# Placing the side tasks of one projection at fixed steps, in a graph-attention layer on one core

## The chip, the core and the metric

The kernel runs on one core of a Trainium2 chip. Times are device microseconds (us) of whole executions. TensorE (PE) multiplies matrices, VectorE (DVE) and ScalarE (ACT) do elementwise work, GpSimd (POOL) does elementwise work and can also issue DMA transfers, SyncE (SP) issues most transfers. Everything is float32.

## The reference, cut to what matters

For each of 128 graphs of 64 nodes: layer norm and relu, four attention heads, a second attention over the joined heads, a feed-forward of two layers, a layer norm and the residual.

```python
Wh = einsum('bnf,hfo->bhno', x, W)
e = leaky_relu(f1[..., :, None] + f2[..., None, :])        # f1, f2: Wh times the two halves of a
attn = softmax(where(adj > 0, e, -1e9), axis=-1)
h = elu(attn @ Wh)                                         # four heads, then once more with W_out
y = relu(out @ w1 + b1) @ w2 + b2 + out
```

## The kernel before

The nodes are cut into 16 groups of four row tiles. Products are done with seven block products in place of eight, so there are weight sums and input sums, and many of them are GpSimd's work. One loop body handles the second projection of group `g` (28 steps on PE of 4 matmul calls each, which the trace lists as 8 instructions, and 1.73 us each) and slips in tasks of other groups. Group 0 has its own list, because the start of the kernel still has work to finish: the first attention of group 0, the softmax of group 1, loads and sums of the feed-forward weights `w1` (M1) and `w2` (M2), norms and softmax of group 2.

```python
def weight_sums(m, after=None):                 # GpSimd: four sums, then two stores of 512 KB
    free = [nc.gpsimd.tensor_tensor(s[0][:, 0], b12, b11, ALU.subtract)]        # L200
    nc.gpsimd.tensor_tensor(s[0][:, 1], b22, s[0][:, 0], ALU.subtract)          # L201
    free.append(nc.gpsimd.tensor_tensor(s[1][:, 0], b22, b12, ALU.subtract))    # L202
    ...
    last = nc.gpsimd.tensor_tensor(s[1][:, 1], b21, s[0][:, 1], ALU.subtract)   # L205
    ...
    for i in range(2):
        nc.gpsimd.dma_start(out=TC[m][i], in_=s[i])                             # L208

def fetch(m, after=None):                       # a whole weight, 1 MB
    queue = nc.scalar if m == 0 else nc.sync if m < H else nc.gpsimd
    ins = queue.dma_start(out=MT[m], in_=mats[m].rearrange("(k p) o -> p k o", p=P))   # L166
...
# softmax of the head weights, VectorE; ei is a tile in SBUF, pe one in PSUM
nc.vector.tensor_tensor(ei, pe[:, i:i + n], mask, ALU.add)                       # L429
nc.vector.scalar_tensor_tensor(ei, ei, ALPHA, ei, ALU.mult, ALU.max)             # L435
nc.vector.tensor_reduce(mi, ei, AX.X, ALU.max)                                   # L436
nc.vector.tensor_tensor(ei, ei, mi[...], ALU.subtract)                           # L437
...                                                                              # exp on ScalarE, sum, 1/sum
nc.vector.tensor_tensor(A[:, u, 0:H], ei[...], ri[...], ALU.mult)                # L443
nc.vector.tensor_copy(A[:, u, H], A[:, u, 0])                                    # L448
```

PE then transposes the weights `A` (L485), and the attention of group 1 is built from them. The other GpSimd work in the stage: L672 adds two blocks of the hidden values, L688 takes differences of blocks for the second projection (each waits until PE has read the block that it overwrites), L314 to L316 are sums of the attention's result `z`, L334 and L344 the scale and shift of a norm.

A scheduler orders each engine's instructions; the kernel steers it by the order of the calls and by `behind(ins, other, reason)`.

## Time and profile before

| | before |
|---|---|
| execution, median of 3 | 2320.97 us (2320.66 to 2322.14) |
| span of the profiled execution | 2318.7 us |
| PE busy | 2279.3 us, 98% |
| PE idle from 100 to 190 us | 16.9 us |
| granted PE clock from 100 to 190 us | 0.91 |

In a kernel in which PE is busy nearly always, a stretch of idle time can be seen only when one asks for PE's own waits. The idle time is the 90 us of that stretch less the 73.06 us in which PE is busy; 14.08 us of it are one gap. The prediction shows the lines.

### The profile page before, as it was taken

What the parts mean: (1) busy time and instruction counts of PE and PEld (TensorE: products, weight loads), DVE (VectorE), ACT (ScalarE), POOL (GpSimd) and SP (SyncE); (2) the same over time, 40 slices, a digit from 0 to 9 for tenths busy, and PEclk for the clock granted to TensorE, in tenths of its full rate; (3) what the DMA queues carried; (4) which work ended last, traced back from release to release, by engine and by line L of the source; (5) the groups of instructions that cost most, each with busy time, mean ns of one, the idle gap of its engine ahead of it and who ended that gap; (6) DMA issues with size and microseconds to landing.
All of it is one profiled execution on the core that took longest, in us unless ns stands there. A gap on an engine that the chain in (4) does not pass through costs nothing. (4 is left out here: it accounts for less than half of the span.)

```text
span 2318.7 us, 33251 instructions
## 1 busy us (share of the span) xinstructions
PE 2279.3 (98%) x11856; PEld 1893.2 (82%) x11856; DVE 1288.4 (56%) x2227; ACT 903.3 (39%) x1629; POOL 1017.0 (44%) x907
## 2 busy tenths in 40 slices
PE   8889999999999999999999999999999999999997
PEld 4568888888888888888888888888888888888885
DVE  7545475555646555475555646555465554744427
ACT  3425425253352534425254252533525244251512
POOL 7742544426344353444425444253443525533324
PEclk9989999999999999999999999999999999999999
DMA  7634454454545445454454545445453454635543
GB/s 277 222 110 134 134 183 136 155 162 134 182 132 177 132 146 178 135 181 132 146 175 133 185 133 159 155 139 181 134 177 130 148 177 132 182 119 165 166 146 105
DMA packets 255011, 361.14 MB, mean 156 GB/s; under 512 B 23768, under 2 KB 143608, under 8 KB 254848
## 3 DMA queue, kind: packets, MB, share of 16 engines
q1 hardware_dynamic: 249744, 341.16, 46.4%
q0 software_dynamic: 4576, 16.81, 2.0%
q8 instruction: 96, 1.57, 0.3%
q10 hardware_dynamic: 528, 1.05, 0.1%
q14 instruction: 67, 0.55, 0.1%
HBM read 331.66 MB, written 27.26 MB: 155 GB/s over the span
## 5 line engine op out<-in xcount | busy, mean ns | idle before, releaser
L304 PE MATMUL g_b<-w,h 128*128 128x256 f32 x2560 | 593.7, 379 | 0.0
L304 PEld LDWEIGHTS g_b<-w,h 128*128 128x128 f32 x2560 | 481.0, 190 | 65.0 <-issue 2.5
L289 PE MATMUL g_a<-z,w 128*128 128x256 f32 x1440 | 341.9, 380 | 0.0
L289 PE MATMUL g_a<-zs_z,w 128*128 128x256 f32 x1440 | 336.0, 381 | 0.0
L289 PEld LDWEIGHTS g_a<-zs_z,w 128*128 128x128 f32 x1440 | 269.9, 190 | 59.2 <-issue 24.3
L289 PEld LDWEIGHTS g_a<-z,w 128*128 128x128 f32 x1440 | 272.3, 190 | 41.3 <-DVE g_a L603 5.0
L304 PE MATMUL g_b<-w,hS 128*128 128x256 f32 x1024 | 240.0, 381 | 0.0
L607 POOL TENSOR_TENSOR hS<-hS,h 128x512 f32<-128x512 f32 x60 | 78.0, 1299 | 360.5 <-DVE hS L573 360.5
L304 PEld LDWEIGHTS g_b<-w,hS 128*128 128x128 f32 x1024 | 193.6, 192 | 25.3
L571 ACT ACTIVATE exc<-g_a 128x512 f32<-128x512 f32 x240 | 142.5, 594 | 163.7 <-DVE g_a L603 95.9
L573 DVE SCALAR_TENSOR_TENSOR h<-exc,g_a 128x512 f32<-128x512 f32 x180 | 123.5, 686 | 140.8 <-ACT exc L572 140.2
L572 ACT ACTIVATE exc<-exc 128x512 f32<-128x512 f32 x240 | 151.4, 631 | 6.6
L314 POOL TENSOR_TENSOR zs_z<-zS,z 128x512 f32<-128x512 f32 x60 | 85.1, 1419 | 139.4 <-PE g_a L289 135.5
L688 POOL TENSOR_TENSOR h<-h,h 128x512 f32<-128x512 f32 x64 | 86.8, 1364 | 135.1 <-PE g_b L304 135.1
L688 POOL TENSOR_TENSOR h<-hS,h 128x512 f32<-128x512 f32 x64 | 81.1, 1268 | 142.6 <-PE g_b L304 142.6
L489 ACT COPY at<-s1pt 128x512 f32<-128x512 f32 x64 | 34.6, 589 | 279.3 <-PE s1pt L485 279.3
L830 POOL TENSOR_TENSOR xr<-xr,bs 128x512 f32<-128x512 f32 x64 | 96.8, 1517 | 78.1 <-DMA xr<-in_x_dram 45.5
L304 PE MATMUL g_d<-w,rt 128*128 128x256 f32 x512 | 121.8, 380 | 2.3 <-DVE o L822 1.0
L289 PE MATMUL g_c<-ot,w 128*128 128x256 f32 x512 | 122.7, 382 | 0.6 <-DVE ot L792 0.6
L289 PE MATMUL g_a<-zS,w 128*128 128x256 f32 x480 | 113.4, 379 | 0.0
L304 PEld LDWEIGHTS g_d<-w,rt 128*128 128x128 f32 x512 | 96.9, 190 | 17.4 <-DVE o L822 2.3
L712 DVE SCALAR_TENSOR_TENSOR jf<-wh,ao 128x512 f32<-128x512 f32 x128 | 97.3, 795 | 24.3 <-ACT wh L694 24.2
(164 smaller groups left out, 3549.1 us busy)
## 6 DMA issues: line engine op xcount, KB each, us to landing
w<-tc SPq DMA_DIRECT2D x624, 256.0 KB, 2.6
w<-in_L_gnn_W_out_dram SPq DMA_DIRECT2D x192, 256.0 KB, 2.7
w<-in_L_gnn_W_heads_dram SPq DMA_DIRECT2D x180, 256.0 KB, 3.0
w<-in_L_gnn_w_dram SPq DMA_DIRECT2D x96, 256.0 KB, 2.7
x<-in_x_dram SPq DMA_DIRECT2D x64, 256.0 KB, 3.7
xr<-in_x_dram SPq DMA_DIRECT2D x128, 128.0 KB, 2.7
out_dram<-o SPq DMA_DIRECT2D x128, 128.0 KB, 2.4
tc<-pt POOLq DMA_DIRECT2D x20, 512.0 KB, 4.3
```

The lines of the kernel that those rows point to most:

```text
L289: LAST["pe"] = nc.tensor.matmul(bk[:, o, :], w[:, k, ts(o, P)], a[:, k, :], start=start and o == 0 and k == 0, stop=k == 1, skip_group_che ...
L304: LAST["pe"] = nc.tensor.matmul(bk[:, j, :], a[:, k, ts(j, P)], w[:, k, :], start=start and k == 0 and j == 0, stop=i == len(ms) - 1 and k ...
L314: eng.tensor_tensor(s2, s1, a11, ALU.subtract)
L489: nc.scalar.copy(AT[t].rearrange("p b h n -> p (b h) n"), pt)
L571: nc.scalar.activation(ex, src, AF.Relu, scale=-1.0)
L572: nc.scalar.activation(ex, ex, AF.Exp, scale=-1.0)
L573: nc.vector.scalar_tensor_tensor(dst, ex, -1.0, src, ALU.add, ALU.max)
L607: nc.gpsimd.tensor_tensor(dst, dst, H1["22"][:, h], ALU.add)
L688: nc.gpsimd.tensor_tensor(dst[:, h], x0[:, h], x1[:, h], ALU.subtract)
L712: nc.vector.scalar_tensor_tensor(junk, WH2[g][:, j], 1.0, ao[:, c, :], ALU.mult, ALU.mult, accum_out=f[:, c, j:j + 1],)
L830: nc.gpsimd.tensor_tensor(xr, xr, bs, ALU.add)
```

## The change

The intent: every side task gets the step of the product behind which it stands. The sums of `w1` go behind the softmax of group 1, the transposes of that softmax two steps later, the load and sums of `w2` later, the norms of group 2 ahead of the sums of `z`.

```diff
-        if g < 2:                                   # the factor R: ScalarE, else VectorE and GpSimd
+        if g < 3:
...
-                if t < G:                           # transposes not ahead of the last product step
+                if t < 2 * G:
...
-    sums_of(M1, LAST["hw", 3, 0])                   # load and sums
+    fetch(M1, LAST["hw", 3, 0])                     # the load alone
...
-        lambda: (attend0(2, 1), turn0(1, 1)), lambda: (attend0(3, 1), turn0(2, 1), project_f(1)),
-        lambda: turn0(3, 1), lambda: (scores1(1), attn_weights(2)), nothing, lambda: attn_weights(3),
-        lambda: (fetch(M2, LAST["hw", 3, 3]), weight_sums(M2, LAST["pe"])), nothing,
-    ] + turns[1:] + [nothing] * 2
...
+                2: lambda: (turn0(3, 1), scores1(1), attn_weights(2), attn_weights(3)),
+                5: lambda: weight_sums(M1, LAST["pe"]),
+                7: turns1[1],
+                8: lambda: fetch(M2, LAST["pe"]),
...
+                13: lambda: (attn[3](), norms[1]()),
+                15: scores[0],
+                16: scores[1],
+                17: lambda: weight_sums(M2, LAST["pe"]),
...
+                22: lambda: z_sums(g + 1, 0),
+                24: turns[1],
+                27: lambda: (turns[4](), load_rows()),
```

## The prediction

> **What bounds the kernel now.** First the page's busy table and its slices. TensorE (PE) is the bound almost everywhere, and the only weak spot ahead of the tail is in the first three slices (a slice is 2318.7 / 40 = 58 us); in the third, from 116 us, the granted clock is down too, to 8 tenths. So the question is where PE waits, not how busy the others are.
>
> ```profile
> PE 2279.3 (98%) x11856; PEld 1893.2 (82%) x11856; DVE 1288.4 (56%) x2227; ACT 903.3 (39%) x1629; POOL 1017.0 (44%) x907
> ...
> PE   8889999999999999999999999999999999999997
> ...
> PEclk9989999999999999999999999999999999999999
> ```
>
> Then the waits of PE alone, over the whole span. One wait dwarfs the rest: the transposes of the attention weights (L485) for the softmax's last multiply (L443). The 6.6 us is the kernel's start, which the change does not touch; the 2.4 us (transposes of normalized rows for a PSUM copy on ScalarE) lies in the same stage, the second projection of group 0.
>
> ```profile
> PE s1pt L485 <- DVE s1A L443: 14.3, 2, 14.1
> PE pab L177 <- DMA ar<-in_L_gnn_a_heads_dram: 6.6, 1, 6.6
> PE pth L362 <- ACT hT L364: 2.4, 1, 2.4
> PE g_c L289 <- ACT t_c L255: 1.1, 1, 1.1
> ```
>
> Then the order in time of PE, VectorE (DVE) and GpSimd (POOL) around that wait (columns: start, duration, engine, line, operation; the bracket is the idle time before it). PE:
>
> ```profile
> 106.37 3.62 PE L304 MATMUL g_b<-w,hS 128*128 128x256 f32 x16
> 124.06 1.94 PE L485 MATMUL s1pt<-ident,s1A 128*128 128x128 f32 x8 [14.08 <-DVE s1A L443]
> 125.80 4.64 PE L304 MATMUL g_b<-w,hS 128*128 128x256 f32 x16
> ...
> 162.08 1.97 PE L362 MATMUL pth<-ident,hn 128*128 128x128 f32 x8 [2.39 <-ACT hT L364]
> 163.84 2.67 PE L304 MATMUL g_b<-w,hS 128*128 128x256 f32 x8
> ```
>
> VectorE in the same time: the leaky-relu step of the softmax takes 14.76 us where the 32 of its line and shape have a median of 0.69.
>
> ```profile
> 105.36 14.76 DVE L435 SCALAR_TENSOR_TENSOR s1e<-s1e 128x512 f32<-128x512 f32 x1
> 120.16 0.69 DVE L436 TENSOR_REDUCE s1mx<-s1e 128x8 f32<-128x512 f32 x1
> ```
>
> GpSimd runs without any idle time from 103.66 to 119.5: differences of the hidden blocks (L672, L688) and the sums of a weight (L200 to L205). VectorE's step ends 0.6 us after the last of them.
>
> ```profile
> 103.66 1.28 POOL L688 TENSOR_TENSOR h<-hS,h 128x512 f32<-128x512 f32 x1
> ...
> 113.44 1.25 POOL L200 TENSOR_TENSOR pt<-pw 128x512 f32<-128x512 f32 x1
> ...
> 118.32 1.25 POOL L205 TENSOR_TENSOR pt<-pw,pt 128x512 f32<-128x512 f32 x1
> 119.53 1.10 POOL L208 DMA_DIRECT2D tc<-pt  x2
> ```
>
> **What the Trainium skill says.** "SBUF — State Buffer", section "Who interferes with whom": a VectorE instruction with two SBUF inputs contends with a GpSimd instruction that reads SBUF, and the one that comes second blocks fully. L435 reads the same SBUF tile twice, so it is of that kind; the 14.76 us beside 0.69 agrees. That it is passed over at twelve boundaries between GpSimd instructions is not what the page leads one to expect, nor usual here: in the later stages the two engines take turns (at 290.01 an L315 of VectorE took 1.64 us, one GpSimd instruction's length longer). "TensorE: Matmul & The Clock Gate", "What's actually happening": an idle window of about 3.4 us halves the clock, and about 3.4 us of work restores it. The trace agrees in kind: 8 transposes took 1.94 us after the wait and 1.04 elsewhere, 16 matmuls 4.64 and 3.62; the granted clock was 0.76 in 124.06 to 132. It also dropped (1.97 us for 8 transposes) after the 2.39 us wait.
>
> **What can be had.** From start to start, so that overlap is not counted twice, 16 matmuls take 3.45 us and 8 transposes 0.87.
> - First wait: 14.08 idle. Afterwards 124.06 to 125.80 is 1.74 for 0.87, and 125.80 to 130.28 is 4.48 for 3.45: 0.87 + 1.03 = 1.90 of slow clock.
> - Second wait: 2.39 idle; 1.76 for 0.87 and 2.60 for 1.73 afterwards: 1.76 (the rest, 0.1, is rounding of start-to-start).
> - Three small waits for the second pair of transposes (178 to 186 us): 0.18 + 0.14 + 0.14 = 0.46.
>
> - A slow issue that counts as busy: the 8 matmuls of the head product L641 at 95.02 take until 96.95, 1.93 where others take 1.02: 0.9.
>
> Sum 14.08 + 1.90 + 2.39 + 1.76 + 0.46 + 0.9 = 21.5 us. From 190 to 2261 us PE has no idle time of 0.1 us, the matmuls are the same number before and after, and from the next stage on the order of instructions is the same in both kernels. So the floor is 2321.0 - 21.5 = 2299.5 us, a gain of 0.9%. 2% would be 46 us, and is not there.
>
> **The change part by part.**
> 1. *The sums of the first feed-forward weight leave the front of the softmax.* Before, they hold GpSimd from 95.49 to 101.6 (four of 1.27 and two DMA issues of 0.55), so the four sums L672 and the differences L688, ready from about 87 us on, queue up behind them and then run as one block. In the changed order they stand behind the second difference of the fifth product. GpSimd then keeps up with PE, and each L688 waits for its own matmuls: PE steps take 1.73, the L688 takes 1.27, so there are holes of 0.4 us and more in which VectorE gets the port. My estimate with before's durations: scores are done at 103.7 instead of 104.5 (the same work stands in front of them, but the head product that was slow comes one step later), L435 starts at 104.5, waits for one L672 to 105.1, ends at 105.7; L437 ends at 107.5; L443 starts at about 109.1, takes turns with GpSimd and ends at 110.9, L448 at 112.2.
> 2. *Two more steps of the product go in front of the transposes.* Before, the transposes stand behind the second hS step; now behind the fourth. That is 2 x 1.73 = 3.45 us more cover: PE arrives at 109.2 + 3.45 = 112.6, after the softmax. First wait: 14.08 to about 0.
> 3. *The sums of the second weight go to step 17*, 4 x 1.25 + 1.1 = 6.1 us out of the block of 103 to 120. The first weight's sums take their place, though: three of them start at about 110.6, and run beside the second softmax of group 1. Its L435, L437, L443 and L448 then take turns, at 0.5 to 1.1 us each: it ends at about 120, against 122.5 at which PE wants it. But the copies of z stand behind it on VectorE, and PE wants one at 120.6. Left over: 0.3 us.
> 4. *Norms ahead of the sums of z.* Before, six z sums (7.5 us) and a L688 hold GpSimd until 158.6, the norms' scale comes after them, and ScalarE's copies wait for it; that is the 2.39. In the changed order both norms stand ahead of the six. From the end of step 13: statistics 1.7, GpSimd's four small ones 1.8, ScalarE to 4.4; PE wants the first transposes at 5.4, the next at 8.0. Second wait and its slow clock: 4.15 to 0.
> 5. *Group 2's factor R on ScalarE instead of VectorE and GpSimd*: four of 0.38 in place of 0.41 + 1.04, done 15.7 us after step 13, against 16.8 at which PE wants it. Nothing, but it keeps R from waiting behind the sums of the second weight.
> 6. Those sums fall at 15.1 to 20.1 us on that scale, and the softmax of group 2 begins at 17.8: 0.6 to 2 us of delay, of which the four steps in front of the transposes (6.9 us for a softmax of 5.5) hide 1.4. The second half has eight score products (L712, 0.68) woven in: 0.3 to 1.5 us of wait.
>
> Left over: 0 + 0.3 + about 1 = 1.3, and 0.3 for a transpose that follows its rows closely at 101.6: 2299.5 + 1.6 = 2301. Such countings leave out waits more often than they invent them, and so I add 3: **2304 us**.
>
> **Rivals.**
> - *VectorE is passed over again.* If L443 or the second L435 meets the first weight's sums and is passed over until they end at about 116.6, the transposes come at 118 instead of 112.6: 5.4 us and 1.9 of slow clock, 2308 to 2309. For: it happened at 105.36, and the sums start on a PE step, not on the softmax. Against: of the 128 instructions L712, also with two SBUF inputs, many beside GpSimd, the longest took 1.76.
> - *The wait moves to group 2*: part 6 goes to its worst, and a wait over 2.4 us costs clock too. 2304 to 2306.
> - *The wait is something else's*, weights not landed for instance, and the softmax was only last. Against: the fifth product's weights were issued at 90 to 93 us, and land in 2.6. 2317 or more; under 5%.
>
> **Range and chances.** Low end is the floor, rounded to 2299.5; the first rival with a little of the second gives the high end, 2310. Executions agree within 1.5 us (2320.66 to 2322.14), so noise adds little. Faster by over 2% would need twice what is idle; slower by over 2% would need a new wait of 46 us.
>
> **What would show it.** Right: no L435 of the first 200 us over 2.5 us; PE's wait for s1A from 14.3 to under 2; no wait for hT at the norms; the granted clock of 100 to 190 us from 0.91 to 0.98 or more; the next stage (g_a, now at 184.2) starting 16 to 20 us sooner, and the same distance at the end. Wrong: an L443 or L435 of 5 us or more that ends with a L205; idle PE in front of the second pair's transposes; a new wait for z.

## The result, and the profile after

The changed kernel took 2299.46 us (median of 4, 2298.54 to 2299.75), against 2320.81 for the kernel before with its newer run counted in. The ratio is 0.9907, 95% interval 0.9890 to 0.9924. A ratio is the mean time of one kernel's fast runs over that of the other's of the same rounds, so it is not quite the ratio of the medians. All outputs are right.

The page of the changed kernel: busy times, and the slices with the granted clock. Before, PE's row began with 888; of these three dips the first, which holds the kernel's start, is left. The dip of the clock is gone.

```profile
PE 2274.2 (99%) x11856; PEld 1892.9 (82%) x11856; DVE 1278.8 (56%) x2226; ACT 904.4 (39%) x1633; POOL 1019.9 (44%) x906
...
PE   8999999999999999999999999999999999999997
...
PEclk9999999999999999999999999999999999999999
```

PE's waits: what was 14.3 us for the softmax is 0.5, and the 2.4 us for ScalarE's copy is gone. The wait at the kernel's start is what it was.

```profile
PE pab L177 <- DMA ar<-in_L_gnn_a_heads_dram: 6.8, 1, 6.8
...
PE s1pt L485 <- DVE s1A L443: 0.5, 1, 0.5
```

PE in order of time. Four hS steps stand in one piece (32 matmuls) in front of the transposes, and nothing is idle: no bracket.

```profile
103.91 1.99 PE L304 MATMUL g_b<-w,h 128*128 128x256 f32 x8
105.74 7.07 PE L304 MATMUL g_b<-w,hS 128*128 128x256 f32 x32
112.65 1.04 PE L485 MATMUL s1pt<-ident,s1A 128*128 128x128 f32 x8
```

VectorE: L435 takes 1.09 us in place of 14.76. It and L437, L443 and L448 each wait for the end of one GpSimd instruction.

```profile
104.74 1.09 DVE L435 SCALAR_TENSOR_TENSOR s1e<-s1e 128x512 f32<-128x512 f32 x1
...
109.17 1.26 DVE L443 TENSOR_TENSOR s1A<-s1e,s1r 128x512 f32<-128x512 f32 x1
110.46 1.17 DVE L448 COPY s1A<-s1A 128x128 f32<-128x128 f32 x1
```

GpSimd: still no idle time that the view would put in a bracket, from 104.01 to 112.7 (pauses of 0.08 us get no bracket). But some of its instructions take 1.6 to 1.7 us, and not 1.27: those are the ones that waited for VectorE in their turn. The load of `w2`, which was issued at 102.86 before, is issued at 121.35.

```profile
104.01 1.27 POOL L688 TENSOR_TENSOR h<-hS,h 128x512 f32<-128x512 f32 x1
105.25 1.72 POOL L672 TENSOR_TENSOR hS<-hS,h 128x512 f32<-128x512 f32 x1
...
121.35 0.77 POOL L166 DMA_DIRECT2D pw<-in_L_gnn_w_dram  x1
```

Where the time came from can be read off one pair of lines: the second product of the next stage, before and after. The first step of the second projection starts at 91.15 us before and 91.22 after.

```profile
187.28 1.89 PE L289 MATMUL g_a<-zS,w 128*128 128x256 f32 x8
```

```profile
165.93 1.89 PE L289 MATMUL g_a<-zS,w 128*128 128x256 f32 x8
```

The stage took 187.28 - 91.15 = 96.1 us and takes 165.93 - 91.22 = 74.7: 21.4 us less, which is the whole gain. From there to the end it is 2318.7 - 187.3 = 2131.4 us before and 2297.4 - 165.9 = 2131.5 after.

### The profile page after: what moved, and what is told of

It reads as the page before. It is cut to its first block, busy times and chain, and to the rows that moved or that the text cites. A ratio compares the mean times of both kernels' runs of the same rounds, so it can differ in the third digit from the quotient of the medians.

```text
span 2297.4 us, 33255 instructions
## 1 busy us (share of the span) xinstructions
PE 2274.2 (99%) x11856; PEld 1892.9 (82%) x11856; DVE 1278.8 (56%) x2226; ACT 904.4 (39%) x1633; POOL 1019.9 (44%) x906
## 5 line engine op out<-in xcount | busy, mean ns | idle before, releaser
L688 POOL TENSOR_TENSOR h<-h,h 128x512 f32<-128x512 f32 x64 | 86.8, 1365 | 138.6 <-PE g_b L304 138.6
L688 POOL TENSOR_TENSOR h<-hS,h 128x512 f32<-128x512 f32 x64 | 81.7, 1277 | 146.7 <-PE g_b L304 146.4
L315 POOL TENSOR_TENSOR zs_z<-z,zs_z 128x512 f32<-128x512 f32 x60 | 81.2, 1353 | 65.1 <-PE g_a L289 44.4
```

The lines of the kernel that those rows point to most:

```text
L315: eng.tensor_tensor(s4, a12, s2, ALU.subtract)
L688: nc.gpsimd.tensor_tensor(dst[:, h], x0[:, h], x1[:, h], ALU.subtract)
```

## The experiments

The open question after the result: the lines agree with the prediction, but it had named the block of GpSimd's work as the cause, and in the changed kernel GpSimd's work at 104 to 113 us is again without a visible hole, and VectorE gets its turns all the same. What differs? Two candidates: the sums of `w1` in front (part 1 of the prediction), and the load that GpSimd issued itself just ahead of the block.

**x1: the sums back in front, the rest as changed.**

```diff
     fetch(M1, LAST["hw", 3, 0])
+    weight_sums(M1, LAST["nb"])
...
-                5: lambda: weight_sums(M1, LAST["pe"]),
```

> The changed kernel with one thing undone: the sums of the first feed-forward weight stand again in front of the softmax (directly behind the weight's load), all else as changed. Theory A (GpSimd's unbroken block holds the port; the sums in front are what makes the block): the sums hold GpSimd from 95.5 to 101.6 us again, the differences then run as one block to about 112, the leaky-relu step L435 starts at 104.7 and is passed over to the end of the block (7 us or more), PE waits 4 to 6 us for the transposes and loses 1.9 of clock: 2305 to 2308 us. Theory B (VectorE is passed over only where GpSimd has issued a DMA of its own shortly before, as with the load of the second weight at 102.86 in the kernel before; that load now comes later): L435 takes 1.0 to 1.8 us, the softmax is done at 112 to 113, PE waits under 0.5 us: 2299.3 to 2300.3 us, as the changed kernel.

Measured: 2299.84 us (2298.35 to 2300.62), ratio 0.9912 to before, as the changed kernel. GpSimd is busy from the sums right into the softmax, with no more than pauses of 0.08 us (from 102.09 + 1.27 = 103.36 to 103.44 in its order in time), and L435 (VectorE's order in time) takes 1.70 us.

```profile
102.09 1.27 POOL L672 TENSOR_TENSOR hS<-hS,h 128x512 f32<-128x512 f32 x1
103.44 1.27 POOL L688 TENSOR_TENSOR h<-hS,h 128x512 f32<-128x512 f32 x1
```

```profile
103.56 1.70 DVE L435 SCALAR_TENSOR_TENSOR s1e<-s1e 128x512 f32<-128x512 f32 x1
```

So the place of these sums is not what cost the time, and theory A falls as it was put. Whether such short pauses matter is left for the later runs.

**x2: the kernel before, with the load of w2 issued by SyncE.**

```diff
-        queue = nc.scalar if m == 0 else nc.sync if m < H else nc.gpsimd
+        queue = nc.scalar if m == 0 else nc.sync if m < H or m == M2 else nc.gpsimd
```

> The kernel before with one thing changed: the load of the second feed-forward weight is issued from SyncE's queue instead of GpSimd's, so that no DMA issue of GpSimd stands in front of its block of differences and sums at 103 to 120 us. Theory A (unbroken block alone): L435 again 13 to 15 us, PE's wait 14 us, time as before within 1 us. Theory B (GpSimd's own DMA issue just ahead is needed): L435 1.0 to 1.8 us, the first half of the softmax done at 111 to 113 us, PE's wait for it 2 to 4 us instead of 14; the second wait (2.4 us with its clock) stays: 2307 to 2312 us.

Measured: 2308.93 us (2307.49 to 2309.69) against 2321.1 for before in the same rounds: 12.2 us by one queue. GpSimd has the same sums and differences in the same stretch; L435 takes 0.89 us. PE's waits for the softmax shrink from 14.3 us to 1.2 + 0.6 + 0.3, and the second wait stays.

```profile
105.41 0.89 DVE L435 SCALAR_TENSOR_TENSOR s1e<-s1e 128x512 f32<-128x512 f32 x1
```

```profile
PE pth L362 <- ACT hT L364: 2.4, 1, 2.4
PE s1pt L485 <- DVE s1A L443: 1.2, 2, 1.0
```

**x3: the changed kernel, with the load of w1 put where the harm was.** Its sums come as late as in the changed kernel; the load is issued at 102 us and not at 87.

```diff
-    fetch(M1, LAST["hw", 3, 0])
...
-                2: lambda: (turn0(3, 1), scores1(1), ...
+                2: lambda: (fetch(M1, LAST["pe"]), turn0(3, 1), scores1(1), ...
```

> The changed kernel with the load of the first feed-forward weight issued by GpSimd at step 2 of the second projection (about 102 us, shortly ahead of the softmax) instead of at 87 us. Theory A (unbroken block alone): the load costs GpSimd 0.8 us, its block has few holes less, L435 takes 1 to 3 us, PE waits under 1 us: 2299.3 to 2301 us. Theory B (a DMA issue of GpSimd just ahead makes it keep the port): L435 or L437 takes over 4 us and is let in only where GpSimd goes idle or issues the next DMA, PE waits 3 us or more: 2303 to 2312 us.

Measured: 2303.43 us (2302.91 to 2303.91), 3.6 us over x1 in the same rounds. The harm is back, in part. GpSimd's order in time: the load, then five instructions without a hole, and each at its undisturbed 1.25; at 109.27 the bracket shows 0.32 us of idle time, as an L688 has to wait for PE.

```profile
101.99 0.78 POOL L166 DMA_DIRECT2D pw<-in_L_gnn_w_dram  x1 [1.86 <-PE g_b L304]
102.79 2.50 POOL L672 TENSOR_TENSOR hS<-hS,h 128x512 f32<-128x512 f32 x2
105.24 2.49 POOL L688 TENSOR_TENSOR h<-hS,h 128x512 f32<-128x512 f32 x2
107.69 1.26 POOL L688 TENSOR_TENSOR hS<-h,h 128x512 f32<-128x512 f32 x1
109.27 1.37 POOL L688 TENSOR_TENSOR hS<-h,h 128x512 f32<-128x512 f32 x1 [0.32 <-PE g_b L304]
110.60 1.72 POOL L200 TENSOR_TENSOR pt<-pw 128x512 f32<-128x512 f32 x1
```

VectorE is let in at that hole: L435 starts at 104.57 and ends 4.94 us later, at 109.51. From then on the two take turns (the L200 of 1.72). So it isn't the load's flight that does it: here VectorE is let in while the load is still in flight (it lands 7.7 us after its issue), and in the kernel before it is kept out long after the load has landed (the L200 at 113.44 reads the loaded `w2`, and L435 ends at 120.12). The first time that GpSimd has to wait ends it.

```profile
104.57 4.94 DVE L435 SCALAR_TENSOR_TENSOR s1e<-s1e 128x512 f32<-128x512 f32 x1
```

**x5: the kernel before, with a hole made on purpose.** Two tiny GpSimd operations follow the load of `w2`, the second dependent on the first.

```diff
+    def hole(after):
+        ...
+        behind(nc.gpsimd.tensor_tensor(a, mhalf, mhalf, ALU.mult), after, "at this place")
+        nc.gpsimd.tensor_tensor(b, a, mhalf, ALU.mult)
...
             behind(ins, after, "not in front of what is needed first")
+        if m == M2:
+            hole(after)
```

> The kernel before, with two tiny dependent GpSimd operations (128x1) directly behind GpSimd's load of the second feed-forward weight at 103.6 us, in front of the block. The second waits for the first, which leaves GpSimd without an instruction for about 0.1 us. Nothing else is changed. Theory B1 (after GpSimd issues a DMA its instructions follow each other without letting go of the port, until it has to wait once): L435 0.9 to 1.8 us, the softmax half done at 112 to 114 us, PE's wait for it 2 to 5 us, 2308 to 2313 us. Theory B2 (as long as that load is not finished, or until the next DMA issue, VectorE is passed over, whatever waits there are): L435 again 14 us or more, 2320 to 2322 us.

Measured: 2308.04 us (2306.50 to 2310.20) against 2319.43: 11.4 us faster than before by two more instructions. GpSimd's order shows the load (numbered L164 in this kernel), the pair, 0.08 us between them (104.72 to 104.80), and then an L672 pair of 3.38 us in place of 2.5, in which VectorE has had its turns.

```profile
103.70 0.80 POOL L164 DMA_DIRECT2D pw<-in_L_gnn_w_dram  x1
104.52 0.20 POOL L158 TENSOR_TENSOR holea<-mhalf 128x1 f32<-128x1 f32 x1
104.80 0.19 POOL L159 TENSOR_TENSOR holeb<-holea,mhalf 128x1 f32<-128x1 f32 x1
...
106.17 3.38 POOL L672 TENSOR_TENSOR hS<-hS,h 128x512 f32<-128x512 f32 x2
```

```profile
104.95 1.80 DVE L435 SCALAR_TENSOR_TENSOR s1e<-s1e 128x512 f32<-128x512 f32 x1
```

x5 alone would not tell the hole from the tiny instructions; x3, where a hole alone did it, makes the hole the likelier reading.

**x6, x11, x12: which DMA?** All three are the changed kernel with a useless DMA issued by GpSimd at step 2, where x3 had its load. x6 stores 512 KB (128 partitions with one row of 4 KB each), x12 loads 512 KB in the same form, x11 stores 1 MB in the form of the weight's load (128 partitions with four rows of 2 KB each).

```diff
+        behind(nc.gpsimd.dma_start(out=again, in_=SUMS[7][0]), after, ...)                 # x6
+        behind(nc.gpsimd.dma_start(out=SUMS[7][0], in_=TC[7][0]), after, ...)              # x12
+        behind(nc.gpsimd.dma_start(out=again.rearrange("(k p) o -> p k o", p=P),
+                                   in_=HW[0].rearrange("p h a t -> p h (a t)")), after, ...) # x11
...
-                2: lambda: (turn0(3, 1), scores1(1), ...
+                2: lambda: (store_again(LAST["pe"]), turn0(3, 1), scores1(1), ...
```

> The changed kernel with an additional, useless store (512 KB from SBUF to a scratch in HBM) issued by GpSimd at the place where experiment x3 had its load; the load itself stays at 87 us. It tells whether the issue of any DMA by GpSimd does it, or only a load. Any DMA: L435 4 to 5 us as in x3 (until GpSimd's first wait at about 109), PE waits 2 to 3 us in sum: 2302.5 to 2304.5 us. Only a load: L435 about 1.1 us, no wait of PE: 2299 to 2300.5 us.

> As x6 (useless store issued by GpSimd shortly ahead of the softmax), but in the size and form of the weight's load turned around: 1 MB, 128 partitions with four rows of 2 KB each, from SBUF to HBM. If the size and form of the issue decide (0.78 us of GpSimd instead of 0.56): L435 4 to 5 us as in x3, PE waits 2 to 3 us in sum, 2302.5 to 2304.5 us. If the direction decides (only loads): L435 about 1.1 us, 2299 to 2300.5 us.

> As x6, but the DMA turned around: a load of 512 KB from HBM to SBUF in the form of x6's store (128 partitions with one row of 4 KB each), with the data that is there already. If the direction decides: L435 4 to 5 us, 2302.5 to 2304.5 us. If the size and form decide: L435 about 1.1 us, 2299 to 2300.5 us.

| | DMA | issue on GpSimd | L435 | time |
|---|---|---|---|---|
| x3 | load 1 MB, four rows | 0.78 us | 4.94 us | 2303.43 us |
| x11 | store 1 MB, four rows | 0.78 us | 4.94 us | 2303.40 us (2302.88 to 2304.22) |
| x6 | store 512 KB, one row | 0.56 us | 1.06 us | 2299.97 us (2299.66 to 2300.14) |
| x12 | load 512 KB, one row | 0.56 us | 1.06 us | 2299.30 us (2298.19 to 2301.00) |

x6 alone pointed at "only a load", and that was wrong: x11, a store, does the same as the load, and x12, a load, does nothing. The direction doesn't matter; size or form does. GpSimd's order in x11, then in x6, from the DMA on:

```profile
102.22 0.78 POOL L209 DMA_DIRECT2D again<-hw  x1 [1.85 <-PE g_b L304]
103.01 2.52 POOL L672 TENSOR_TENSOR hS<-hS,h 128x512 f32<-128x512 f32 x2
105.47 2.50 POOL L688 TENSOR_TENSOR h<-hS,h 128x512 f32<-128x512 f32 x2
```

```profile
102.15 0.56 POOL L209 DMA_DIRECT2D again<-pt  x1 [1.85 <-PE g_b L304]
102.73 2.50 POOL L672 TENSOR_TENSOR hS<-hS,h 128x512 f32<-128x512 f32 x2
105.19 3.41 POOL L688 TENSOR_TENSOR h<-hS,h 128x512 f32<-128x512 f32 x2
```

In x6 the two L688 take 3.41 us, as VectorE had turns; in x11 2.50, undisturbed.

x6 and x12 also settle what x1 and x2 leave open. In those two and in the changed kernel GpSimd has pauses of 0.08 us between a L672 and the L688 behind it (x1: 103.36 to 103.44; x2: 101.94 to 102.02), and x5's hole is no longer than that; so they alone could mean that any block of GpSimd without a pause shuts VectorE out. But in x6 and x12 nothing in GpSimd's order starts more than 0.02 us after the end of what stands before it, from the DMA to the boundary at which L435 is let in (105.19 us in x6), and L435 takes 1.06 us. A block without a pause shuts VectorE out only behind the DMA of 1 MB.

**x4: the transposes behind step 5, the rest as changed.**

```diff
-                5: lambda: weight_sums(M1, LAST["pe"]),
-                7: turns1[1],
+                5: lambda: (weight_sums(M1, LAST["pe"]), turns1[1]()),
```

> The changed kernel with the transposes of the first half of group 1's weights behind step 5 again instead of behind step 7 (part 2 undone alone). If the two more steps are needed as cover: PE arrives at 109.2 us, the softmax is done at 110.4 to 111.6, PE waits 1.2 to 2.4 us, with up to 1.8 us of slow clock: 2301 to 2304 us. If the freed port alone brings the gain and the cover nothing: 2299.5 us as the changed kernel.

Measured: 2301.97 us (2301.63 to 2302.22), 2.5 us over the changed kernel. PE waits for this softmax in three pieces, 1.21 + 0.59 + 0.27 = 2.07 us (PE's order in time; another 0.44 us, which its list of waits adds to the first, belongs to group 2, and the changed kernel has it too); the granted clock of the execution stays at 0.999. Part 2 is worth about 2.5 us, once the large wait is gone.

**x7: the second pair of norms behind the sums of z again.**

```diff
-                13: lambda: (attn[3](), norms[1]()),
-                15: scores[0],
+                13: attn[3],
+                15: lambda: (norms[1](), scores[0]()),
```

> The changed kernel with the second pair of norms of group 2 called at step 15 instead of 13, so that in GpSimd's order the six sums of z and two differences stand in front of their scale again (part 4 undone alone). If part 4 is worth what the prediction says or more: GpSimd comes to the norms at about 144 us, ScalarE has the first row tile at 145.8, PE wants it at 139.5: a wait of 5 to 7 us and up to 1.9 of slow clock: 2305 to 2308 us. If PE's wait of before had another cause: 2299.3 to 2300.5 us.

Measured: 2305.89 us (2304.73 to 2306.58). PE has a wait that wasn't there, for the norm's result:

```profile
PE pth L362 <- ACT hn L346: 5.4, 1, 5.4
```

The order of these norms on GpSimd is worth 6.4 us here; in the kernel before it was 2.39 and its slow clock, because PE came there later: it is ready for the transposes of these norms at 159.5 us, when GpSimd has begun the norms at 158.61, and in x7 at 138.7, when GpSimd begins them only at 142.43.

**x8: the factor R on VectorE and GpSimd again.**

```diff
-        if g < 3:
+        if g < 2:
```

> The changed kernel with group 2's factor R made by VectorE and GpSimd again (part 5 undone alone). The prediction's own reading (it keeps R from waiting behind the sums of the second weight): R comes in GpSimd's order behind the four sums and two DMA issues that end at 152.5 us, is done at 153.6, PE wants it at 148.6: 4 to 5.5 us of wait and up to 1.9 of slow clock: 2304 to 2307 us. Rival (R is small and hidden): 2299.3 to 2300.3 us.

Measured: 2305.74 us (2305.47 to 2307.24).

```profile
PE s1pe L405 <- POOL R L391: 5.0, 1, 5.0
```

Part 5 gains nothing against before, but the change needs it: with the sums of `w2` moved to step 17, R would stand behind them.

**x9 and x10: the changed kernel again, and with its last transposes one step later.**

```diff
-                27: lambda: (turns[4](), load_rows()),
+                27: load_rows,
...
                 steps[i % 6]()
+                if g == 1 and i == 0:
+                    turns[4]()
```

> The changed kernel again, unaltered, beside the others on one chip. The prediction's lower end was 2299.5 us (2321.0 less 21.5 of idle and slow PE), and the result was 2299.46. If the executions spread about the floor: median 2298.5 to 2300.5 us, some executions under 2299.5; PE's remaining wait in this stage 0.3 to 0.6 us.

> The changed kernel with the last transposes of group 2's weights one product step later, behind the first step of the next stage (as the scheduler had it in the kernel before), to take away the 0.45 us that PE still waits for the softmax there. Should be 0.3 to 0.8 us below the changed kernel, which is about the spread of the executions; nothing if the wait only moves.

Measured: x9 2298.98 us (2298.82 to 2299.88), x10 2298.74 us (2297.97 to 2299.42). In x10's list of PE's waits the 0.5 us for the softmax is gone, but 0.24 us between medians whose ranges overlap isn't a difference that these runs settle. No version here is shown to beat the changed kernel.

## Why the prediction was right or wrong

The direction and nearly every time in the working were right, and the size of what could be had was close. The range was missed by 0.04 us, 2299.46 against a lower end of 2299.5, because the floor at that end was set too high (22.1 us could be had, not 21.5) and the 3 us of waits that were added did not come. One cause was named wrongly, and that the size came out all the same was luck in that part.

**The sum was near before 3 us were added to it.** The counting gave 2301, 1.5 us over the result; "such countings leave out waits more often than they invent them, and so I add 3" is the step that failed for the centre. No such wait exists in the changed kernel: from 100 to 190 us the only wait in PE's list is 0.45 us, at the second transposes of group 2 (part 6: "0.3 to 1.5").

**The floor was taken for a wall.** It stood at 2321.0 - 21.5, and the range's low end was put on it. Two things were wrong with that. The waits were counted as idle time, 14.08 and 2.39, while the slow matmuls behind them were counted from start to start. From start to start the waits are 124.06 - (106.37 + 3.45) = 14.24 and 162.08 - (157.79 + 1.73) = 2.56, 0.33 us more. And executions spread by about 1.2 us (2298.54 to 2299.75), which belongs on both sides of a floor. In x10, with no wait left, the stage takes 164.45 - 90.39 = 74.06 us against 96.13 before: 22.1 us could be had, of which 21.5 + 0.33 is accounted for and 0.2 isn't.

**Part 1 failed as a cause.** Its step was that the sums of `w1` in front make the differences "run as one block", and that holes of 0.4 us in which VectorE gets the port are what helps. x1 has the sums in front and costs nothing. The holes of 0.4 us did not come either: the changed kernel has L672 and L688 close together at 104 to 111 us, with pauses of at most 0.08 us, and they take turns with VectorE. What decided was not named at all: GpSimd issued the load of `w2` at 102.86 and had no hole until the block's end. x2 takes only that away and gets 12.2 of the 21.3 us. `w1` and `w2` share one buffer (the tag `out`), so the load of `w2` cannot come before the sums of `w1`; when the change moved these sums to step 5, the load had to follow them, and the cure came along with the move. The prediction had noticed that being passed over again and again (it says at twelve boundaries; it is twelve instructions, so eleven) was not usual in this trace, and went on as if it were: that was the place to stop and ask. Its example of the usual was read a little long: the L315 of 1.64 us is 0.95 us over the undisturbed 0.69, the rest of the GpSimd instruction that was running, not the length of one.

**Its times came out.** Predicted: L435 from 104.5 to 105.7, L443 done at 110.9, L448 at 112.2, PE at 112.6. Measured: 104.74 to 105.83, 110.43, 111.63, 112.65. They held because the working let VectorE take turns, as it does once the load is elsewhere.

**Part 2** was given 3.45 us of cover, and x4 measures 2.5 us for taking it away. **Part 3** left 0.3 us: PE's only trace of it is 2.15 us for the 16 attention matmuls at 117.07 and 1.18 for the 8 transposes at 123.00, about 0.1 to 0.2 us each more than their siblings. **Part 4** was right: no PE wait at the norms, clock from 0.91 to 1.00 over 100 to 190 us. **Part 5** was right in both halves (x8: 5.0 us of wait). **Part 6** was right in size. The rivals did not come: in the changed kernel no VectorE instruction of that softmax takes over 1.3 us.

Added up from different runs: 12.2 (x2), 2.5 (x4), 2.39 + 1.76 (the second wait and its clock in the kernel before), 0.9 for the slow head product and 0.46 for the three small waits, 20.2 of 21.35 us. The rest isn't assigned, and such pieces need not add up exactly.

## What to carry to other kernels

When one instruction takes twenty times its siblings' time, ask what is different there from the places where the same neighbours do no harm, before building on the neighbour. Where VectorE is on the critical path and works beside GpSimd, try moving a large DMA issue of GpSimd away from the front of its gap-free work; another queue for the one load was worth 12 us here, and a dependent pair of tiny instructions nearly as much. A counted sum needs a range on both sides, not padding on one.

## What the Trainium skill lacked or had wrong

- "SBUF — State Buffer", section "Who interferes with whom": it has the lock, and that the second to come blocks until the first is done. It lacks who is next. Ordinarily VectorE is let in at the next boundary between GpSimd instructions (L435 0.89 to 1.80 us in the changed kernel, x1, x2, x5, x6 and x12). After GpSimd has issued a DMA of 1 MB with four rows of 2 KB a partition, it is passed over at every boundary until GpSimd has a hole: 4.94 us in x3 and x11, 14.76 us over eleven boundaries in the kernel before (twelve instructions of GpSimd), where no hole came and it was let in as GpSimd issued its next DMA. A DMA of 512 KB with one row a partition doesn't do it (x6, x12: 1.06 us).
- The same page, section "SBUF: two separate sides", warns of VectorE holding up GpSimd's descriptors. The reverse, an issue of GpSimd that makes VectorE wait afterwards, is on no page that I found. Why it happens no run here shows: whether size, number of rows or the longer issue (0.78 against 0.56 us) decides is open, and so is whether a hole of 0.08 us is enough without the tiny instructions of x5.
- "TensorE: Matmul & The Clock Gate", section "What's actually happening": the table gives an idle window of about 3.4 us for the slow clock. Here the slow clock also followed an idle time of 2.39 us (8 transposes 1.97 us in place of 1.04), and one of 2.40 us in x2, where it set in behind the transposes (8 matmuls 3.58 us in place of 1.89), while three pieces of 1.59, 0.60 and 0.27 us with transposes between them (x3) left the clock at 0.999.
